# First-layer cross attention: where the exponentials and their sums are made

## The chip, the cores and the metric

The kernel runs on one core of a Trainium2 chip. A core has a matrix engine (PE, with PEld for its weight loads), VectorE (DVE), ScalarE (ACT), GpSimd (POOL) and SyncE (SP), which issues most transfers. Each engine works through its own instructions in order; semaphores hold an instruction back until its operands are there. The metric is the device time of one execution in microseconds.

## The reference

The model is a decoder of two layers over 32 sequences of 128 tokens, 128 features wide, with a context of 77 keys for each sequence. Layer 0 is retention, cross attention and a mixture of 8 experts; layer 1 is a memory, a differential cross attention and a second mixture. The change is in the cross attention of layer 0 alone. The reference cut to it:

```python
q = decoder_output @ wq_w + wq_b          # 16 heads of 8 features
k = encoder_output @ wk_w + wk_b
v = encoder_output @ wv_w + wv_b
score = jnp.einsum('bhqd,bhkd->bhqk', q, k) / jnp.sqrt(8.0)
score = score * mask
score = jnp.where(score == 0, NEG_INF, score)
alignment = jax.nn.softmax(score, axis=-1)
context = jnp.einsum('bhqk,bhkd->bhqd', alignment, v)
heads = context.reshape(b, -1, 128) @ wo_w + wo_b
```

## The kernel before, in words

All arithmetic is fp32. The 32 sequences are taken in eight groups of four (G = 4). The 77 keys are padded to S2 = 78 by repeating the last key, so that four heads of 78 keys make 312 columns, which fall into three strided parts of 104.

For one sequence the attention has two steps. `weigh(n)` (L528) works with the 128 queries on the partitions. GpSimd spreads the keys by head into `km` (L531). PE makes the scores `csc` of 16 heads in four products (L541). VectorE multiplies them by the mask into `ph` (named `prob` in the profile, 128 x 16 x 78, L543), makes the penalty `z` (L549), adds it (L550), takes the maximum over the keys for each query and head (`mx`, L552), and subtracts it (L553).

`read(n, ph)` (L556) turns that to keys on the partitions. PE makes 12 transposes of 104 x 128 into `ptp` (L564), and ScalarE takes the exponential on the way from PSUM to `pT`, two instructions of 104 x 768. `attend` (L488) then makes two sets of 12 products with `pT` (L494, each 32 rows of output): one with the values `vb` for the numerator, and one with the constant `vmask`, zeros and ones, for the sum of the exponentials. The sums are inverted by `power` (L155), a logarithm and an exponential on ScalarE, and VectorE multiplies (L574) into `oT`. The values and the mask both have a zero in the row of the repeated key.

`expln` (L149) is a helper through which the activations are issued, so all exponentials and logarithms have line L139 in the profile.

`cross0` (L576) runs these steps one sequence ahead: `weigh(n + 1)` is issued before `read(n)`. The stage is woven by `beside` (L1414) with other work: the retention (`retention`, L370) and query, key and value products (`prepare0`, L506) of groups ahead, and the output product, layer norms and routing (`joined0`, `route`) of the group behind, then the scatter of its tokens to the experts (`dispatch`, L646). The order on each engine is not the source's: a scheduler of the framework places the instructions by its own estimate of when each can run, so an edit to one step can move others.

Names in the trace that the steps below use: `yn` (L462) is the normed retention output; `po_ro` its product with the output weights; `ry` (L465) the sum with the input; `x` from `ry` (L317) the layer norm after it; `cqT` and `ckT` the queries and keys; `rqT` and `rkT` those of retention, `qm` (L391) GpSimd's spread of `rqT`, `rsc` the retention scores, `rt` (L411) the scores times the decay, `py` (L425) their product with the values and `yr` (L433) its copy; `xT_ln` a transposed layer norm; `place` (L664) the rows to which tokens are scattered; `pvc` (L475) the value products.

Tiles come from pools with few buffers. `prob` has three, which `ph` and `z` share; `pair` has two, and the scores, the transposes and the retention scores take turns in it. A step that holds one of these long keeps others from starting.

Of the kernel before, what the change touches and what calls it, by code (L numbers as in the profile page):

```python
# [10 lines left out]
F32 = mybir.dt.float32  # L11
I32 = mybir.dt.int32
U32 = mybir.dt.uint32
AF = mybir.ActivationFunctionType
ALU = mybir.AluOpType
AX = mybir.AxisListType

P = 128
B, S, D = 32, 128, 128
S2 = 78  # L20
# [7 lines left out]
KT = 26  # L28
# [81 lines left out]
def kernel(ctx: ExitStack, tc: tile.TileContext, a: dict, at: dict):  # L110
    nc = tc.nc
    cp = ctx.enter_context(tc.tile_pool(name="const", bufs=1))
    st = ctx.enter_context(tc.tile_pool(name="stream", bufs=2))
    wk = ctx.enter_context(tc.tile_pool(name="work", bufs=2))
    sm = ctx.enter_context(tc.tile_pool(name="small", bufs=4))
# [4 lines left out]
    def bank(name):  # L120
        return ps.tile([P, 512], F32, tag="bank", name=name)

    def pair(name):
        return pp2.tile([P, 2, 512], F32, tag="pair", name=name)

    def bank3(name):
        return bank(name).rearrange("p (b f) -> p b f", b=G)
# [4 lines left out]
    def by_table(table, out, x, func, **kw):  # L132
        if stretch["table"] != table:
            load = nc.scalar.add_instruction(
                mybir.InstLoadActFuncSet(name=nc.get_next_instruction_name(), act_func_set_id=table, ins=[], outs=[])
            )
            in_order(load, stretch["used"])
            stretch.update(table=table, load=load, used=[])
        act = nc.scalar.activation(out, x, func, **kw)  # L139
        in_order(act, [stretch["load"]])  # L140
        stretch["used"].append(act)
# [7 lines left out]
    def expln(out, x, func, **kw):  # L149
        by_table(EXP_LN, out, x, func, **kw)  # L150
# [4 lines left out]
    def power(out, x, p, bias=0.0):  # L155

        expln(out, x, AF.Ln, bias=bias)
        expln(out, out, AF.Exp, scale=p)
# [9 lines left out]
    def c_(name):  # L168
        return cst[:, at[name][0] : at[name][1]]
# [24 lines left out]
    def load_context(g):  # L194

        c4 = st.tile([P, G, 4, S2], F32, tag="c4", bufs=1, name=f"c4{g}")
        nc.sync.dma_start(c4, a["ctx4"][g])
        return c4
# [286 lines left out]

    vmask = c_("vmask").rearrange("p (t d) -> p t d", t=3)

    def attend(chunk, vb, num, den):  # L488

        for out, lhs in ((num, vb), (den, vmask)):  # L490
            for t in range(3):
                for j in range(4):
                    js = slice(32 * j, 32 * j + 32)
                    nc.tensor.matmul(  # L494
                        out[js, :],
                        lhsT=lhs[: 4 * KT, t, js],
                        rhs=chunk(j, t),
                        start=(t == 0),
                        stop=(t == 2),
                        skip_group_check=True,  # L500
                    )


    served = {}
# [23 lines left out]
    def weigh(n):  # L528
        qT, kT, _, mk, _ = served[n]
        km = wk.tile([P, 4, S2], F32, tag="km", name="km0")  # L530
        nc.gpsimd.tensor_tensor(  # L531
            km,
            kT.unsqueeze(1).broadcast_to([P, 4, S2]),
            c_("kmask0").unsqueeze(2).broadcast_to([P, 4, S2]),
            ALU.mult,
        )
        ph = wk.tile([P, 16, S2], F32, tag="prob", bufs=3, name="prob0")
        pscs = [pair("csc") for _ in range(2)]
        for r in range(4):
            rr = slice(32 * r, 32 * r + 32)  # L540
            nc.tensor.matmul(pscs[r // 2][:, r % 2, : 4 * S2], lhsT=qT[rr, :], rhs=km[rr, :, :], start=True, stop=True)  # L541
        for k in range(2):
            nc.vector.tensor_mul(  # L543
                ph[:, 8 * k : 8 * k + 8, :].rearrange("p (r h) k -> p r h k", r=2),
                pscs[k][:, :, : 4 * S2].rearrange("p r (h k) -> p r h k", h=4),
                mk.unsqueeze(1).unsqueeze(1).broadcast_to([P, 2, 4, S2]),
            )
        z = wk.tile([P, 16, S2], F32, tag="prob", bufs=3, name="z")
        nc.vector.tensor_scalar(z, ph, 0.0, NEG_INF, ALU.is_equal, ALU.mult)  # L549
        nc.vector.tensor_add(ph, ph, z)  # L550
        mx = sm.tile([P, 16], F32, tag="mx", name="mx0")
        begun.append(nc.vector.tensor_reduce(mx, ph, AX.X, ALU.max))  # L552
        nc.vector.tensor_tensor(ph, ph, mx.unsqueeze(2).broadcast_to([P, 16, S2]), ALU.subtract)  # L553
        return ph

    def read(n, ph):  # L556
        _, _, vb, _, oT = served.pop(n)
        pT = wk.tile([P, 2, 2, 3, S], F32, tag="pT", bufs=4, name="pT0")
        for k in range(2):
            pt = pair("ptp")  # L560
            for i in range(2):
                for t in range(3):
                    h0 = 8 * k + 4 * i
                    nc.tensor.transpose(  # L564
                        pt[: 4 * KT, i, t * S : (t + 1) * S],
                        ph[:, h0 : h0 + 4, :].rearrange("p h k -> p (h k)")[:, t::3],
                        ident,
                    )
            expln(pT[: 4 * KT, k].rearrange("p i t s -> p i (t s)"), pt[: 4 * KT, :, : 3 * S], AF.Exp)
        acc = bank3("pav0")  # L570
        attend(lambda j, t: pT[: 4 * KT, j // 2, j % 2, t, :], vb, acc[:, 0, :], acc[:, 1, :])
        rd = wk.tile([P, S], F32, tag="rd", name="rd0")
        power(rd, acc[:, 1, :], -1.0)
        nc.vector.tensor_mul(oT, acc[:, 0, :], rd)  # L574

    def cross0():  # L576

        ph = weigh(0)
        yield
        for n in range(B):  # L580
            ahead = weigh(n + 1) if n + 1 < B else None
            yield
            read(n, ph)
            yield
            ph = ahead
# [349 lines left out]
    def keys1(g, c4):  # L935
        pk = bank("dpk")[:, : G * S2]
        nc.tensor.matmul(pk, lhsT=w_("L1_xattn_Wk"), rhs=c4[:, :, 0, :], start=True, stop=True)
        kT = wk.tile([P, G, S2], F32, tag="ckT", name="dkT")
        nc.scalar.copy(kT, pk.rearrange("p (b k) -> p b k", b=G))
        yield  # L940
        km, vbs = [], []
        for b0 in range(0, G, 2):
            pair_km = wk.tile([P, 2, 8, S2], F32, tag="prob", bufs=3, name="km1")
            for i in range(2):
                nc.gpsimd.tensor_tensor(
                    pair_km[:, i],
                    kT[:, b0 + i, :].unsqueeze(1).broadcast_to([P, 8, S2]),
                    c_("kmask1").unsqueeze(2).broadcast_to([P, 8, S2]),
                    ALU.mult,
                )  # L950
                km.append(pair_km[:, i])
            for i in range(2):
                vbs.append(values(c4, b0 + i, 1))
            yield
        keyed[g] = km, vbs
# [420 lines left out]
    def after0(g, fine=False):  # L1376
        x2 = yield from joined0(g, held.pop(("x1", g)), held.pop(("oT", g)), fine)
        yield
        yield from route(g, x2, fine)
# [74 lines left out]
    last = [after0(NG - 1, True), dispatch(NG - 1, 1, other_tiles), keys1(0, load_context(0))]  # L1454
# [62 lines left out]
```

## Time and profile before

| | us |
|---|---|
| Median of 3 runs | 1583.14 |
| Lowest and highest | 1569.38 and 1587.96 |
| Profiled execution | 1564.15 |
| Its span, first to last instruction | 1562.3 |
| First exponential of the attention by key, start | 71.8 |
| Last product of `pav` in this attention, start | 544.2 |
| PE busy | 1221.8 |
| VectorE busy | 784.1 |
| ScalarE busy | 490.6 |
| GpSimd busy | 466.5 |

The profiled execution is some 19 us below the median. Each profile row names a line, an engine, an operation, the tile written and read, its shapes and a count, then busy microseconds and mean nanoseconds of one, then the idle time of the engine before it and what ended that. A matrix product in fp32 appears as two records. Times in the time line count from the start of the span.

### The profile page before, as it was taken

Reading aid. Unit: us, or ns where it says so; the run is one execution under the profiler, and the core shown is the slowest. Engines: PE = TensorE matmul, PEld = TensorE weight load, DVE = VectorE, ACT = ScalarE, POOL = GpSimd, SP = SyncE. Lnnn points to the kernel's source line nnn. Section 1 sums busy time; section 2 is a strip of 40 time slices with the busy share of each in tenths; the row PEclk is TensorE's granted clock in tenths of the full one; section 3 lists DMA queues with packets and bytes.
Section 4 is the critical chain, followed back from the end, with each engine's and each line's share of the span. In section 5 each row is a group of like instructions: output and inputs, shape, how many; then the busy total and the mean of one; then the engine's idle time right before and its main releaser. Section 6 shows DMA issues by size and latency. Waiting matters only on the chain.

```text
span 1562.3 us, 27821 instructions
## 1 busy us (share of the span) xinstructions
PE 1221.8 (78%) x11445; PEld 910.3 (58%) x11445; DVE 784.1 (50%) x2174; ACT 490.6 (31%) x1036; POOL 466.5 (30%) x451
## 2 busy tenths in 40 slices
PE   4788777778777789899796998888989999527840
PEld 3556555555555578788674665656666666316430
DVE  2678767676576734222333435535445354376212
ACT  3235243332334424233231232432424334200113
POOL 0110131321214465554635303123011010004762
PEclk8798788776788689899895788988989999656975
DMA  3322221120211235455521101011011000001335
GB/s 113 105 75 76 75 76 53 64 89 21 75 48 65 91 125 174 148 181 186 155 87 46 38 2 51 22 42 44 30 48 30 23 15 16 14 0 25 68 31 121
DMA packets 75599, 107.21 MB, mean 69 GB/s; under 512 B 13840, under 2 KB 60944, under 8 KB 75472
## 3 DMA queue, kind: packets, MB, share of 16 engines
q0 software_dynamic: 19088, 53.63, 12.1%
q1 hardware_dynamic: 56384, 51.80, 10.7%
q8 instruction: 90, 1.47, 0.4%
q14 instruction: 37, 0.30, 0.1%
HBM read 65.80 MB, written 39.60 MB: 67 GB/s over the span
## 4 chain that ended last, share of the span: by engine, by line
PE 52%; DVE 19%; issue 9%; POOL 8%; ACT 5%; DMA 4%; another core or an unknown queue 3%; POOLq 0%; SPq 0%; ACTq 0%; DVEq 0%
PE pgu L810 6%; PE pav L1015 5%; PE dsc L963 5%; PE dst L987 4%; PE dst L998 3%; PE pav L494 3%; PE pd L825 3%; PE pvc L475 3%; PE ptp L564 2%; POOL total L1331 2%; PE csc L541 2%; DVE top L965 2%; DVE x L320 2%; PE py L425 2%
## 5 line engine op out<-in xcount | busy, mean ns | idle before, releaser
L965 DVE TENSOR_REDUCE top<-dsc 128x4 f32<-128x312 f32 x256 | 111.5, 476 | 139.8 <-PE dsc L963 128.3
L139 ACT ACTIVATE pT<-dst 104x768 f32<-104x768 f32 x128 | 96.5, 806 | 237.9 <-PE dst L998 224.1
L810 PE MATMUL pgu<-tT,wt 128*128 128x256 f32 x624 | 152.6, 391 | 7.0 <-ACT tT L792 6.3
L963 PE MATMUL dsc<-km,dqT 32*128 32x312 f32 x512 | 121.4, 520 | 31.7 <-DVE top L965 22.5
L810 PEld LDWEIGHTS pgu<-tT,wt 128*128 128x128 f32 x624 | 116.3, 195 | 25.5 <-ACT tT L792 11.7
L816 DVE TENSOR_TENSOR sg<-sg,pgu 128x512 f32<-128x512 f32 x78 | 53.5, 686 | 151.6 <-ACT sg L139 142.3
L987 PE MATMUL dst<-dqT,km 32*104 32x128 f32 x1536 | 119.2, 337 | 7.1 <-ACT pT L139 6.3
L671 POOL DMA_INDIRECT xslot<-z,place x64 | 70.2, 1097 | 146.2 <-DVE place L664 107.0
L987 PEld LDWEIGHTS dst<-dqT,km 32*104 32x104 f32 x1536 | 98.6, 228 | 20.5 <-ACT pT L139 11.1
L825 PE MATMUL pd<-wt,sg 128*128 128x128 f32 x624 | 88.7, 288 | 16.6 <-DVE sg L816 12.0
L963 PEld LDWEIGHTS dsc<-km,dqT 32*128 32x128 f32 x512 | 50.3, 200 | 85.7 <-DVE top L965 49.2
L564 PE MATMUL ptp<-cst,prob 128*104 128x128 f32 x384 | 74.2, 342 | 32.5 <-DVE gbi L457 23.8
L825 PEld LDWEIGHTS pd<-wt,sg 128*128 128x128 f32 x624 | 81.7, 200 | 22.3 <-DVE sg L816 15.4
L998 PE MATMUL dst<-mT,cst 32*104 32x128 f32 x1536 | 87.6, 299 | 2.9 <-issue 2.9
L531 POOL TENSOR_TENSOR km<-ckT,cst 128x312 f32<-128x312 f32 x32 | 22.7, 720 | 216.4 <-PE csc L541 151.0
L564 PEld LDWEIGHTS ptp<-cst,prob 128*104 128x104 f32 x384 | 60.3, 189 | 41.5 <-issue 34.6
L998 PEld LDWEIGHTS dst<-mT,cst 32*104 32x104 f32 x1536 | 78.3, 185 | 4.5 <-issue 4.4
L139 ACT ACTIVATE sg<-pgu 128x512 f32<-128x512 f32 x78 | 46.6, 597 | 97.7 <-PE pgu L810 80.1
L541 PE MATMUL csc<-km,cqT 32*128 32x312 f32 x256 | 61.1, 560 | 18.8 <-POOL km L531 13.0
L475 PE MATMUL pvc<-wv,c 128*104 128x128 f32 x384 | 69.0, 336 | 5.3 <-DVE top L965 3.9
L475 PEld LDWEIGHTS pvc<-wv,c 128*104 128x104 f32 x384 | 63.7, 242 | 14.2 <-DVE top L965 8.5
L857 POOL DMA_INDIRECT two<-xslot,place x64 | 61.9, 968 | 32.0 <-issue 16.3
(351 smaller groups left out, 2450.3 us busy)
## 6 DMA issues: line engine op xcount, KB each, us to landing
xslot<-zero SPq DMA_DIRECT2D x75, 256.0 KB
c<-in_ctx SPq DMA_DIRECT2D x16, 624.0 KB
wt<-in_experts SPq DMA_DIRECT2D x16, 192.0 KB
xg<-in_x SPq DMA_DIRECT2D x8, 256.0 KB
accrow<-fh SPq DMA_DIRECT2D x8, 256.0 KB
facc<-accrow SPq DMA_DIRECT2D x8, 256.0 KB
xrow<-x SPq DMA_DIRECT2D x8, 256.0 KB
total<-x SPq DMA_DIRECT2D x8, 256.0 KB
```

The costliest lines, as they stand in the source:

```text
L139: act = nc.scalar.activation(out, x, func, **kw)
L475: nc.tensor.matmul(pv[: 4 * KT, t, :], lhsT=c4[:, b].rearrange("p h k -> p (h k)")[:, t::3], rhs=wv[:, layer, :], start=True, stop=True,)
L541: nc.tensor.matmul(pscs[r // 2][:, r % 2, : 4 * S2], lhsT=qT[rr, :], rhs=km[rr, :, :], start=True, stop=True)
L564: nc.tensor.transpose(pt[: 4 * KT, i, t * S : (t + 1) * S], ph[:, h0 : h0 + 4, :].rearrange("p h k -> p (h k)")[:, t::3], ident,)
L671: put = nc.gpsimd.indirect_dma_start(out=xslot, out_offset=bass.IndirectOffsetOnAxis(ap=place[:, k, g * G + b : g * G + b + 1].bitcast(U32 ...
L810: nc.tensor.matmul(pgu[:, i, c * TB * P : (c + 1) * TB * P], lhsT=w[:, at_w : at_w + P], rhs=x, start=True, stop=True)
L825: nc.tensor.matmul(pd[:, b, :], lhsT=sgs[c0 // 2][:, c, b, :], rhs=w[:, at_w : at_w + D], start=(c0 + c == 0 and b == 0), stop=(c0 + c == ...
L963: nc.tensor.matmul(banks[w][:, : 4 * S2], lhsT=qT[rr], rhs=km[rr, 4 * k : 4 * k + 4, :], start=True, stop=True)
L965: nc.vector.tensor_reduce(tops[n % 3][:, w, 4 * k : 4 * k + 4], banks[w][:, : 4 * S2].rearrange("p (h k) -> p h k", h=4), AX.X, ALU.max,)
L987: nc.tensor.matmul(pts[w // 2][: 4 * KT, w % 2, t * S : (t + 1) * S], lhsT=km[rr, 4 * k : 4 * k + 4, :].rearrange("p h k -> p (h k)")[:, t ...
L998: nc.tensor.matmul(pts[w // 2][: 4 * KT, w % 2, t * S : (t + 1) * S], lhsT=fold[rr], rhs=mT[rr, :], start=False, stop=(t == 2), skip_group ...
L1015: nc.tensor.matmul(out[js], lhsT=lhs[: 4 * KT, t, js], rhs=pTs[j % 2][: 4 * KT, :, j // 2, t, :], start=(t == 0), stop=(t == 2), skip_grou ...
```

## The change

The exponentials are taken before the transposes, with the queries still on the partitions. VectorE negates the maxima. ScalarE then makes one exponential for each head, 128 x 77, in place, with the negated maximum as the bias and the sum over the keys as a second output. VectorE inverts the 16 sums of each query and multiplies the weights by them. The transposed weights are then only copied from PSUM by ScalarE. `attend` makes one set of 12 products, with the values; the set with `vmask` is gone here, though the second layer still has one. ScalarE copies the result to `oT`. The 78th column, the repeated key, is not exponentiated and stays a scaled score; it meets a zero row in the values.

```diff
-    def attend(chunk, vb, num, den):
-        for out, lhs in ((num, vb), (den, vmask)):
-            for t in range(3):
-                for j in range(4):
...
+    def attend(chunk, vb, out):
+        for t in range(3):
+            for j in range(4):
...
-        nc.vector.tensor_tensor(ph, ph, mx.unsqueeze(2).broadcast_to([P, 16, S2]), ALU.subtract)
+        nc.vector.tensor_scalar(mx, mx, -1.0, None, ALU.mult)
+        last = S2 - 1
+
+        sums = sm.tile([P, 16], F32, tag="sums0", name="sums0")
+        for h in range(16):
+            expln(ph[:, h, :last], ph[:, h, :last], AF.Exp, bias=mx[:, h : h + 1], accum_out=sums[:, h : h + 1])
+        nc.vector.reciprocal(sums, sums)
+        nc.vector.tensor_mul(ph, ph, sums.unsqueeze(2).broadcast_to([P, 16, S2]))
         return ph
...
-            expln(pT[: 4 * KT, k].rearrange("p i t s -> p i (t s)"), pt[: 4 * KT, :, : 3 * S], AF.Exp)
-        acc = bank3("pav0")
-        attend(lambda j, t: pT[: 4 * KT, j // 2, j % 2, t, :], vb, acc[:, 0, :], acc[:, 1, :])
-        rd = wk.tile([P, S], F32, tag="rd", name="rd0")
-        power(rd, acc[:, 1, :], -1.0)
-        nc.vector.tensor_mul(oT, acc[:, 0, :], rd)
+            nc.scalar.copy(pT[: 4 * KT, k].rearrange("p i t s -> p i (t s)"), pt[: 4 * KT, :, : 3 * S])
+        acc = bank("pav0")[:, :S]
+        attend(lambda j, t: pT[: 4 * KT, j // 2, j % 2, t, :], vb, acc)
+        nc.scalar.copy(oT, acc)
```

More of the change, by code (lines that the diff above doesn't have):

```diff
@@ L486 @@
     vmask = c_("vmask").rearrange("p (t d) -> p t d", t=3)
-    def attend(chunk, vb, num, den):
-        for out, lhs in ((num, vb), (den, vmask)):
-            for t in range(3):
-                for j in range(4):
[L493 to L501, printed above, removed]
+    def attend(chunk, vb, out):
+        for t in range(3):
+            for j in range(4):
+                js = slice(32 * j, 32 * j + 32)
+                nc.tensor.matmul(
+                    out[js, :],
+                    lhsT=vb[: 4 * KT, t, js],
+                    rhs=chunk(j, t),
+                    start=(t == 0),
+                    stop=(t == 2),
+                    skip_group_check=True,
+                )
     served = {}
```

## The prediction

> **What bounds the kernel now.** I read first where first-layer attention lies (the windows by stage), then the chain that ended last inside it, then the groups of instructions that the edit touches, and last one group of four sequences in order of time, because only that shows what a longer step on ScalarE would push.
>
> The windows cut the stage at the row maxima of successive groups; columns are length, then busy time of PE, PEld, DVE, ACT and POOL, granted clock, DMA share, GB/s.
>
> ```profile
> 183.80:248.00 64.20, 48.60 (x474) 35.75 (x474) 47.14 (x126) 25.03 (x59) 17.26 (x16) 0.85 0.22 71
> 248.00:317.00 69.00, 53.28 (x472) 38.85 (x472) 47.48 (x122) 24.79 (x59) 17.82 (x16) 0.77 0.20 66
> ...
> sum 488.00, PE 378.32 PEld 276.12 DVE 353.10 ACT 181.55 POOL 122.02; mean PE 54.05 PEld 39.45 DVE 50.44 ACT 25.94 POOL 17.43
> ```
>
> The stage runs from 58 to 546 us: 488 us for 32 sequences. PE is busy 78% of it, VectorE 72%, ScalarE 37%. No engine is full; the stage is a chain that hops between PE, VectorE and ScalarE. The groups that the edit touches or that price it:
>
> ```profile
> L139 ACT ACTIVATE pT<-ptp 104x768 f32<-104x768 f32 x64 | 50.4, 804 | 59.7 <-PE ptp L564 59.2 <-PE pt_ln L346 0.5
> L553 DVE TENSOR_TENSOR prob<-prob,mx 128x1248 f32<-128x1248 f32 x32 | 46.9, 1466 | 0.4
> L494 PE MATMUL pav<-pT,vb 104*32 104x128 f32 x768 | 39.8, 327 | 0.8 <-ACT pT L139 0.7
> L494 PE MATMUL pav<-pT,cst 104*32 104x128 f32 x768 | 34.7, 306 | 0.0
> L317 ACT ACTIVATE x<-ry,nb_l0a,r_l0a 128x128 f32<-128x128 f32 x32 | 13.2, 482 | 2.2 <-DVE mv_l0x L308 1.7 <-DVE nb_l0a L312 0.5
> L139 ACT ACTIVATE rd<-rd 128x128 f32<-128x128 f32 x32 | 9.8, 307 | 0.8
> L350 ACT COPY xT_c<-pt_c 128x512 f32<-128x512 f32 x16 | 9.3, 584 | 24.9 <-PE pt_c L346 24.6
> L139 ACT ACTIVATE rd<-pav 128x128 f32<-128x128 f32 x32 | 8.9, 277 | 121.9 <-PE pav L494 95.4 <-PE pvc L475 14.2 <-remote 12.3
> L976 ACT COPY mT<-pt_mx 128x128 f32<-128x128 f32 x32 | 8.4, 263 | 8.3 <-PE pt_mx L974 8.3
> ```
>
> Here ScalarE waits for PE (121.9 us before rd alone), not the reverse. In the chain inside 58 to 546 us, L494 is the largest line, 10.2% (50 us). Half of its products are the mask products (pav<-pT,cst). One group, in order of time:
>
> ```profile
> 246.46 1.45 DVE L552 TENSOR_REDUCE mx<-prob 128x16 f32<-128x1248 f32 x1
> 251.79 1.64 ACT L462 ACTIVATE yn<-yr,gbi,gsc 128x128 f32<-128x128 f32 x4
> 260.57 1.65 ACT L317 ACTIVATE x<-ry,nb_l0a,r_l0a 128x128 f32<-128x128 f32 x4 [0.29 <-DVE mv_l0x L308]
> 266.05 0.99 POOL L671 DMA_INDIRECT xslot<-z,place  x1 [22.53 <-DVE place L664]
> 285.73 0.57 ACT L379 COPY rqT<-pq 128x512 f32<-128x512 f32 x1
> 288.52 1.45 DVE L552 TENSOR_REDUCE mx<-prob 128x16 f32<-128x1248 f32 x1
> ```
>
> Call its sequences A to D. ScalarE carries the layers woven in beside them: yn and x (the next groups), rqT and the key and value copies (retention two groups on). All are on the way to PE's next work.
>
> **The change, part by part.** *Removed:* 768 mask matmul records, 34.7 us of PE busy, 1.1 per sequence; they stand on the chain, so at most 25 us (half of 50). The subtraction, 1.466, is replaced by a multiplication of one shape, also taken as 1.466. rd's two activations (0.277 + 0.307) and the 0.28 product give way to one 128x128 copy from PSUM, 0.263 by L976. The wide Exp becomes a copy of one shape: 0.80 before; the copy rows L976 and L350 rise 0.836 ns per element, so 0.80 after.
>
> *Added, small:* a negation and a reciprocal of 128x16 on VectorE; the nearest rows are its 128x4 and 128x8 ones, 0.15 to 0.2 each. Less the product gone, VectorE's sum hardly moves.
>
> *Added, large:* 16 Exp of 128x77 per sequence with a pointer for the bias and an accumulator. L317 gives the form nearest: four in a row take 1.65, one 0.482, so the pitch is (1.65-0.482)/3 = 0.389. Take off 51 elements (0.043) and the second pointer (0.08, from 128x4 rows with and without one, 0.287 and 0.201): 0.267. No row has an accumulator. The lower bound is 0.267, a free one. Upper: no overlap (0.287 + 73 x 0.836 ns = 0.348) plus a small instruction to fetch the sum (0.2): 0.55. I take 0.42, between them, since the sum exists only after the last element: 0.348, no overlap, and 0.07 for handing it over. That is 6.7 us per sequence, 215 in all, and brings ScalarE to about 390 of 488 us.
>
> The Trainium skill, "ScalarE: Activation LUTs", section "What ACT_TABLE_LOAD costs", states 280 ns plus 0.833 per element with a pointer, and 93 ns overlap: 0.251 here. It speaks against sixteen narrow instructions, most of each being fixed cost, but names no price for the accumulator. By its 0.251 the sum below ends at -19 us (a gain); by my 0.42 at +35. Rows here agree with the formula at 0.267; the difference is the accumulator.
>
> **What lies beside and what on the path.** In the changed order VectorE runs A's maximum, B's mask, z and maximum, and only then A's reciprocal and multiplication, so most of A's exponentials are covered there. But ScalarE is in order, and what stands behind each block waits. I walk the group with 0.42, in the changed order of each engine:
> - A's block runs 248.3 to 255.0. yn is behind it: 256.7 instead of 253.4 at its end. po_ro, then ry, 258 instead of 256.6.
> - B's first ten stand before r_l0a: x starts 262.6 instead of 260.6; six more lie among the two layer norms, so the context keys end 268.6 instead of 265.7. VectorE's place is +3.3, hence POOL's eight scatters and the key products queued behind them (276.9 before) begin 3 us later. SP's zero fills are released by the maxima and its order hardly moves.
> - A's copies of the transposes come only after B's block: products for A end 273, C's scores follow, C's maximum ends 281.2 instead of 274.6. This lateness is partly absorbed, for D's scores stood behind POOL in the kernel before.
> - C's block runs 283.6 to 290.3. Behind it is rqT, 290.9 instead of 286.3, then POOL's qm and PE's rsc. D's maximum ends 295.5 instead of 290.0, the rt pair 298 instead of 293.7.
> - D's block runs 297.1 to 303.8; behind it yr, xT_ln and C's copies, to 306.6. The mask products that filled 303.3 to 305.2 here are gone. The second rt pair ends 313 instead of 308.6.
>
> So a group is 4.4 us longer, with the removed products already out. Eight groups: +35 us. About 2.5 of the four blocks lie on the path, so 0.01 us on each Exp is 0.4 us per group, 3.2 us in all. At 0.267 the sum is 35 - 0.153 x 320 = -14; at 0.55 it is 35 + 0.13 x 320 = +77. The later stages (experts, second attention) keep their instructions; the start of the stage and its end, where experts join, are counted as groups like the others.
>
> The profiled execution took 1564.15 us (span 1562.3); with the sum, about 1599. The median shown is 1583.14, 19 above it, so the forecast for the median is 1583 + 35 = 1618. 1% is 16 us, about what a measurement of this kernel can tell from no change.
>
> **The rivals.**
> 1. *ScalarE becomes the bound* (0.2). The accumulator costs an instruction of its own, 0.55 each: 282 us more, 453 busy of 488, and all four waits bite. For: yn, rqT, yr and the copies stand behind blocks. Against: 306 us of idle time now. +77: 1660.
> 2. *Faster* (0.18). The accumulator is nearly free and the exponentials fit in ScalarE's idle time; then only the 25 us of mask products and the rd chain leave the path. For: ScalarE idles 63% here and PE's L494 leads the chain. It decides from a pitch of 0.31 downward (35/3.2 = 11 hundredths below 0.42). At 0.267: 1583 - 14 = 1569; with more slack at POOL's waits, down to -25: 1558.
> 3. *Nothing measurable* (0.22). The blocks cost what the products gave, at a pitch of 0.31 to 0.36: 1583 to 1599.
> 4. *The forecast* (0.4): 1618, itself within about 1600 to 1640.
>
> The range must reach into 1 and 2: 1567 to 1670. Faster 0.18, same 0.22, slower 0.6.
>
> **What would show it.** Right: the stage at about 523 us; ScalarE busy near 390 in it; a spacing of about 0.42 between exponentials; yn, rqT and yr waiting on nothing but their own engine; PE's wait for ScalarE (yn, xT_ln, rqT through qm) grown, the mask products' 34.7 us gone. Wrong: a spacing under 0.31, or VectorE's reciprocal held long by ScalarE in every sequence (then more than 2.5 blocks are on the path), or a longer time in the second attention.

## The result, and the profile after

The changed kernel takes 1665.49 us (median of four executions, 1662.38 to 1674.73), against 1578.59 for the kernel before on the same chip: a ratio of 1.0626 [1.0579, 1.0672], some 87 us more. The forecast of +35 us (1618) had the sign, and the time lies inside the range of 1567 to 1670, but the size is far out. On three other chips the same kernel came out 1.0424, 1.0433 and 1.0461 of the kernel before, which itself takes about 1537 us there: 63 to 70 us more. So the experiments below are each compared with what ran on the same chip. On the chip of x1, x3 and x5 two executions of the kernel before were slow ones and are left out of every comparison.

The first row of the page after, and the stage that was 58 to 546 us before (length, then busy time of PE, PEld, DVE, ACT and POOL, granted clock, DMA share, GB/s). It now ends at 643, where the first expert products start:

```profile
span 1673.0 us, 27258 instructions
PE 1247.6 (75%) x10677; PEld 912.1 (55%) x10677; DVE 808.4 (48%) x2206; ACT 653.3 (39%) x2028; POOL 460.8 (28%) x451
```

```profile
58.00:643.00 585.00, 392.99 (x2736) 270.57 (x2731) 379.12 (x921) 344.62 (x1417) 116.66 (x113) 0.68 0.17 55
```

The first expert product (`pgu`) started at 545.9 us before and starts at 642.3 now, 96 us later. The two executions differ by 110.7 us of span, more than the medians do, for the one before lies below all its timed runs and the one after is the slowest of its four. So most of the loss is in this stage. What lies behind it is 14 us longer (1016.4 and 1030.7 us), 13 of them in the second attention (518 and 531 us), with the same instructions. This part is not the edit's: in three traces from one other chip, everything behind the stage takes 982 and 988 us in two variants of the kernel before (x4, x6) and 979 in the changed kernel (after_again).

PE has 757 records fewer in the stage (2736 for 3493) and yet 15 us more of busy time, at a granted clock of 0.68 for 0.79. ScalarE is busy 345 us; the prediction said about 390.

The exponentials in the groups of ScalarE for this stage (busy, mean ns of one, then the idle time before them):

```profile
L139 ACT ACTIVATE prob<-prob,mx 128x77 f32<-128x77 f32 x512 | 176.5, 354 | 20.8 <-DVE mx L552 20.8
L139 ACT ACTIVATION_READ_ACCUMULATOR prob<-prob,mx 128x1 f32 x512 | 100.2, 196 | 0.0
L575 ACT COPY pT<-ptp 104x768 f32<-104x768 f32 x64 | 50.2, 799 | 48.1 <-PE ptp L570 46.0 <-remote 2.0
```

The sum over the keys is an instruction of its own in the records, 196 ns. The time line of the profiled execution (start, duration) shows how it costs less than that:

```profile
257.01 1.44 DVE L551 TENSOR_REDUCE mx<-prob 128x16 f32<-128x1248 f32 x1
262.09 0.36 ACT L139 ACTIVATE prob<-prob,mx 128x77 f32<-128x77 f32 x1
262.35 0.19 ACT L139 ACTIVATION_READ_ACCUMULATOR prob<-prob,mx 128x1 f32 x1
262.44 0.35 ACT L139 ACTIVATE prob<-prob,mx 128x77 f32<-128x77 f32 x1
...
267.25 0.36 ACT L139 ACTIVATE prob<-prob,mx 128x77 f32<-128x77 f32 x1
267.78 0.58 ACT L379 COPY rqT<-pq 128x512 f32<-128x512 f32 x1
268.44 1.04 POOL L391 TENSOR_TENSOR qm<-rqT,cst 128x512 f32<-128x512 f32 x1 [0.28 <-ACT rqT L379]
...
273.84 1.44 DVE L551 TENSOR_REDUCE mx<-prob 128x16 f32<-128x1248 f32 x1
275.21 1.21 DVE L411 TENSOR_TENSOR rt<-rsc,dmat 128x1024 f32<-128x1024 f32 x1
276.34 0.64 DVE L552 TENSOR_SCALAR mx<-mx 128x16 f32<-128x16 f32 x1
277.01 0.36 ACT L139 ACTIVATE prob<-prob,mx 128x77 f32<-128x77 f32 x1 [1.41 <-DVE mx L552]
...
282.17 0.36 ACT L139 ACTIVATE prob<-prob,mx 128x77 f32<-128x77 f32 x1
282.65 0.25 DVE L558 RECIPROCAL sums<-sums 128x16 f32<-128x16 f32 x1 [4.54 <-ACT prob L139]
```

From one exponential to the next it is 0.344 us (262.09 to 267.25 is fifteen of them): the next one starts before the accumulator is read out. A block of 16 takes 5.5 us, not 6.7. The rest of the fence is what the walk of the prediction looked for: rqT stands behind a block and GpSimd's qm behind rqT; at the end VectorE's reciprocal has waited for the block. And something the walk did not have: the fourth sequence's maxima end at 275.28, but the negation stands behind a retention product (`rt`, 1.21 us) on VectorE, so its block starts only at 277.01.

The chain of this stage by line, and four of its waits (total us, times, longest), both of the kernel after:

```profile
by line: ACT prob L139 18.9%; PE csc L540 9.7%; PE pav L493 7.9%; PE ptp L570 6.6%; ACT x L317 3.6%; DVE mx L551 3.5%; DVE prob L542 3.4%; PE rsc L401 3.3%; PE py L425 3.2%; PE pvc L475 2.8%; DVE rt L411 2.6%; DVE prob L549 2.6%; PE po_ro L
```

```profile
DVE sums L558 <- ACT prob L139: 51.2, 17, 5.8
PE po_ro L360 <- ACT yn L462: 48.3, 7, 7.8
POOL qm L391 <- ACT rqT L379: 24.1, 6, 19.7
PE py L425 <- DVE rt L411: 35.6, 12, 5.9
```

Before, the leading line of this chain was PE's L494 with 10.2%; now ScalarE's exponentials lead it with 18.9%. VectorE waits for whole blocks (17 times, up to 5.8 us), and PE's output product of the retention waits for yn, which stands behind a block, 7 us in each of seven groups. In the kernel before, only its weight load is listed as waiting for yn, and shortly:

```profile
PEld po_ro L360 <- ACT yn L462: 5.1, 7, 0.8
```

### The profile page after: what moved, and what is told of

Its sections match the earlier page's. It is cut to its first block, busy times and chain, and to the rows that moved or that the text cites. A ratio compares the mean times of both kernels' runs of the same rounds, so it can differ in the third digit from the quotient of the medians.

```text
span 1673.0 us, 27258 instructions
## 1 busy us (share of the span) xinstructions
PE 1247.6 (75%) x10677; PEld 912.1 (55%) x10677; DVE 808.4 (48%) x2206; ACT 653.3 (39%) x2028; POOL 460.8 (28%) x451
## 4 chain that ended last, share of the span: by engine, by line
PE 54%; DVE 16%; ACT 13%; issue 7%; POOL 5%; DMA 3%; another core or an unknown queue 2%; POOLq 0%; SPq 0%; ACTq 0%; DVEq 0%
ACT prob L139 7%; PE pav L1019 5%; PE pgu L814 5%; PE dsc L967 5%; PE dst L991 4%; PE dst L1002 4%; PE csc L540 3%; PE pav L493 3%; PE pd L829 3%; PE pvc L475 3%; PE ptp L570 2%; POOL total L1335 2%; DVE x L320 2%; DVE top L969 2%
## 5 line engine op out<-in xcount | busy, mean ns | idle before, releaser
L139 ACT ACTIVATE prob<-prob,mx 128x77 f32<-128x77 f32 x512 | 176.5, 354 | 20.8 <-DVE mx L552 20.8
L570 PE MATMUL ptp<-cst,prob 128*104 128x128 f32 x384 | 80.9, 367 | 44.9 <-DVE prob L559 22.4
L829 PE MATMUL pd<-wt,sg 128*128 128x128 f32 x624 | 88.7, 288 | 17.6 <-DVE sg L820 14.7
L139 ACT ACTIVATION_READ_ACCUMULATOR prob<-prob,mx 128x1 f32 x512 | 100.2, 196 | 0.0
L570 PEld LDWEIGHTS ptp<-cst,prob 128*104 128x104 f32 x384 | 64.1, 195 | 59.4 <-issue 29.2
L542 DVE TENSOR_TENSOR prob<-csc,mk 128x624 f32<-128x624 f32 x64 | 50.6, 804 | 60.0 <-PE csc L540 55.7
L475 PE MATMUL pvc<-wv,c 128*104 128x128 f32 x384 | 70.2, 338 | 3.9 <-DVE top L969 3.9
```

Of the source, the lines that this page charges most:

```text
L475: nc.tensor.matmul(pv[: 4 * KT, t, :], lhsT=c4[:, b].rearrange("p h k -> p (h k)")[:, t::3], rhs=wv[:, layer, :], start=True, stop=True,)
L570: nc.tensor.transpose(pt[: 4 * KT, i, t * S : (t + 1) * S], ph[:, h0 : h0 + 4, :].rearrange("p h k -> p (h k)")[:, t::3], ident,)
L829: nc.tensor.matmul(pd[:, b, :], lhsT=sgs[c0 // 2][:, c, b, :], rhs=w[:, at_w : at_w + D], start=(c0 + c == 0 and b == 0), stop=(c0 + c == ...
```

## The experiments

**The parts by themselves.** x4 takes the removal alone: the kernel before without mask products, logarithm, exponential and multiplication of the sums.

```diff
-        for out, lhs in ((num, vb), (den, vmask)):
+        for out, lhs in ((num, vb),):
...
-        power(rd, acc[:, 1, :], -1.0)
-        nc.vector.tensor_mul(oT, acc[:, 0, :], rd)
+        nc.scalar.copy(oT, acc[:, 0, :])
```

> The kernel before with the mask products, the reciprocal and its multiplication left out (the numerator is only copied). It measures what the removed part is worth by itself. By the prediction's step (half of what the chain shows for these products): 20 to 30 us faster, 1550 to 1560. If, as putting them back into the changed kernel suggests, they lie in PE's slack: within 10 us of before.

1509.39 us against 1537.74 on the same chip: 0.9828 [0.9766, 0.989], 28 us less, as expected. The first step of the sum (at most 25 for the products, and what the chain of the sums gives) stands. So the added part costs more than the whole loss shows: if the two parts simply add, 63 + 28 = 91 us on this chip.

x6 does the opposite: it leaves the kernel before as it is and puts ScalarE's new work beside it, on constants that nobody reads.

```diff
+        for h in range(16):
+            expln(junk, zero[:, :77], AF.Exp, bias=mx[:, h : h + 1], accum_out=jsum[:, h : h + 1])
```

> The kernel before with sixteen more exponentials with sums per sequence, of constants, with the maximum as bias, into tiles that nothing reads: ScalarE does the added work, but no transposes wait for it. If ScalarE's in-order queue (what stands behind the blocks) is what costs, most of the 85 us: 1630 to 1660. If it is the weights' longer way (maximum, exponentials, multiplication, transposes), 1585 to 1610.

1569.4 us, 1.0193 [1.0137, 1.0248]: 32 us, at the upper end of the second theory. A full extra load of ScalarE, which the weights themselves do not pass through, costs about a third of 91. The load is even larger than in the changed kernel: where these exponentials follow each other directly, it is 0.48 us from one to the next here, for 0.344 there. They all write one tile, and whether that is the reason was not tried. The framework also spreads these instructions between others, so this is not the price of the load in the places it has in the changed kernel. By subtraction, then, most of the loss is the weights' own longer way; the next two runs test that directly.

x3 keeps that way but takes the block down to one instruction of 128x1248; x2 keeps sixteen instructions and takes only the sums from them. The first part of the diff is x3's, the second x2's.

```diff
-        for h in range(16):
-            expln(ph[:, h, :last], ph[:, h, :last], AF.Exp, bias=mx[:, h : h + 1], accum_out=sums[:, h : h + 1])
-        nc.vector.reciprocal(sums, sums)
+        expln(ph, ph, AF.Exp, bias=mx[:, 0:1])
+        nc.vector.reciprocal(sums, mx)
...
-            expln(ph[:, h, :last], ph[:, h, :last], AF.Exp, bias=mx[:, h : h + 1], accum_out=sums[:, h : h + 1])
-        nc.vector.reciprocal(sums, sums)
+            expln(ph[:, h, :last], ph[:, h, :last], AF.Exp, bias=mx[:, h : h + 1])
+        nc.vector.reciprocal(sums, mx)
```

> The changed kernel with one exponential of 128x1248 per sequence instead of sixteen, with the negated maximum of the first head as bias for all; the sums are left out (the reciprocal is taken of the maxima instead). The hand-overs from VectorE to ScalarE and back stay, the block falls from 5.5 to about 1.3 us. Theory 1 and 2 (the block's length): the stage loses more than it gained, 1545 to 1575, with a clock near 0.79. Theory 3 (the hand-overs themselves and the weights' longer way, not the block): 1600 or more.

> The changed kernel with the sixteen exponentials without their sums (left out; the reciprocal is taken of the maxima). A block should fall from 5.5 us (0.343 each) to about 4.0 (0.25 each). If the length of the blocks sets the time (one exponential of about 1.3 us gave 1550, sixteen with sums 1665, so 27 us per us of block), 1620 to 1635. If the number of the hand-overs or the number of instructions counts and not their length, 1650 or more.

x3 takes 1549.92 us, 0.9854 [0.9778, 0.9931] of the kernel before on its chip: level, within the intervals, with the products simply removed (x4, 0.9828). Its one instruction, in the groups of its ScalarE:

```profile
L139 ACT ACTIVATE prob<-prob,mx 128x1248 f32<-128x1248 f32 x32 | 42.6, 1333 | 10.7 <-DVE mx L552 8.6 <-issue 2.1
```

So an exponential in this place costs nothing beyond the interval, some 12 us, if it is 1.3 us long. (In x3 the negation of the fourth sequence of a group no longer stands behind `rt`, except in the earliest, so its fall from the changed kernel is not the block's alone.)

x2 takes 1557.5 us, 1.0135 [1.0068, 1.0202], and the changed kernel on the same chip (after_again) 1600.91. The sums alone are worth 43 us, within the fall of 30 to 45 (from 1665) that the theory of the block's length gave. The order is no rival here, for the negation of the fourth sequence of a group stands behind `rt` in x2 as well. A block of x2 in its time line:

```profile
251.52 4.10 ACT L139 ACTIVATE prob<-prob,mx 128x77 f32<-128x77 f32 x16
```

(4.10 - 0.35)/15 = 0.25 us from one to the next. So the sum costs 0.094 us on each exponential, 1.5 us on a block and 48 us on 32 of them, of which 43 are seen at the end.

> The changed kernel again, beside the others on one chip: 1655 to 1675.

It came out at 1600.91 us, 1.0424 [1.0359, 1.0488], below what the first chip gave; the excess of about 20 us there came with that chip, and what causes it was not found.

**Is it PE's clock?** With the products gone PE has more idle time in the stage and its records are slower (a score product 628 ns for 560). x5 puts work into that idle time: a bank of PSUM set apart, and 24 unread products ahead of `po_ro` in every fourth sequence. x5_filled_0 sets the bank apart and fills nothing. x1 puts the mask products back, unread. The first part of the diff is x5_filled_24's, the second x1's.

```diff
+        for _ in range(24 if n % 4 == 1 else 0):
+            fill = nc.tensor.matmul(warm[:, :P], lhsT=ident, rhs=dmat[:, 0, :], start=True, stop=True)
+            in_order(fill, [neg])
...
-        attend(lambda j, t: pT[: 4 * KT, j // 2, j % 2, t, :], vb, acc)
-        nc.scalar.copy(oT, acc)
+        attend(lambda j, t: pT[: 4 * KT, j // 2, j % 2, t, :], vb, acc[:, 0, :])
+        attend(lambda j, t: pT[: 4 * KT, j // 2, j % 2, t, :], vmask, acc[:, 1, :])
+        nc.scalar.copy(oT, acc[:, 0, :])
```

> The changed kernel with one PSUM bank set apart (three in turn instead of four) and no filling: the comparison for the filled one. Both theories: 0 to 20 us above the changed kernel, 1665 to 1685, for the lost bank.

> The changed kernel with one PSUM bank set apart and 24 products of 128x128 in it that nothing reads, in every fourth sequence, on PE just ahead of the retention output product, where PE waits some 7 us for the normed retention output behind a block of exponentials. Theory 1 (clock): the filled wait keeps the clock up for the products behind it; useful PE work gets faster and the time is 8 to 25 us below the same kernel without filling, although PE has about 40 us more to do. Theory 2 (waits alone): equal to that kernel within 5 us, or longer.

> The changed kernel with the 12 products with the mask put back for each sequence, into columns of the accumulator that nothing reads. Theory 1 (clock): the changed kernel is slower than forecast because PE, waiting for ScalarE's blocks, is granted a lower clock (0.68 in the stage against 0.79); more products fill PE, the clock rises to 0.71 or more, and the time stays within 10 us of the changed kernel: 1655 to 1675. Theory 2 (the waits behind the blocks alone, the clock plays no part): the products cost what they were taken to give, some 25 us: about 1690.

x5_filled_0 takes 1658.06, x5_filled_24 1685.42. The filling did go where it was meant: the products are there, and `po_ro` waits less for yn.

```profile
L556 PE MATMUL warm<-dmat,cst 128*128 128x128 f32 x384 | 51.3, 300 | 0.0
L362 PE MATMUL po_ro<-wm,yn 128*128 128x128 f32 x56 | 14.3, 345 | 16.8 <-ACT yn L464 16.8
```

In x5_filled_0 the same row reads:

```profile
L362 PE MATMUL po_ro<-wm,yn 128*128 128x128 f32 x56 | 14.1, 425 | 48.3 <-ACT yn L464 48.3
```

The wait fell by 31.5 us (48.3 to 16.8) for 51.3 us of filling, and the mean clock of the stage rose from 0.72 to 0.76; yet the time went up by 27, as the theory of the waits has it. The filling overshot its hole by 20 us, which is most of that; but it gave little back. PE's other work up to the first expert product is 374 us busy for 377. So filling the idle time ahead of `po_ro` does not make PE's other products faster here. (The profiled execution of x5_filled_24 was its fastest, 1670.02 us, so the trace holds only some 10 of the 27 us.)

x1 takes 1647.43 us, 1.0486 [1.0407, 1.0564] on its chip: less than the changed kernel's 1.0626 on the first, with more to do, and less than either theory gave. Side by side on one chip:

> The changed kernel once more, so that the three others of this call can be set against it on one chip: 60 to 90 us above before.

> The changed kernel with the mask products put back unread, now on the same chip as the changed kernel. If PE's clock or its idle time is what the products decide, 0 to 20 us below the changed kernel; if the products are plain cost, as leaving them out of the kernel before gave 28 us, 15 to 30 us above it.

1604.76 and 1575.36 us: 29 us less with the products put back, more than expected. They also change the order in which the framework places other instructions. In x1 the fourth sequence's negation comes right after its maxima, in all groups but the earliest; in the changed kernel it stands behind `rt`. Clock and order are thus two possible causes of one number, and the series with y3 and y5 takes them apart.

**Ends or middle?** In the trace of the result the opening (to the sixth sequence's maxima) is 29 us longer, the five groups after it 49 together, the closing 18. The prediction counted all groups alike. y1 makes the change for sequences 5 to 25 only (shown), y2 for the eleven others, each with the kernel before's form for the rest.

```diff
+    def changed(n):
+        return 5 <= n <= 25
...
+        if not changed(n):
+            nc.vector.tensor_tensor(ph, ph, mx.unsqueeze(2).broadcast_to([P, 16, S2]), ALU.subtract)
+            return ph
```

> The change for the 21 sequences between, the ends as before. If the ends hold half of the loss: 30 to 48 us above before. If every sequence costs alike: 40 to 60 us, two thirds of the changed kernel's loss.

> The change for eleven sequences alone (the first five and the last six); the other 21 as before. The traces lay half of the stage's growth (48 of 97 us) on these ends, where little is woven in beside a block. If so, this kernel is half of the changed kernel's loss above before: 30 to 48 us. If every sequence costs alike, as the prediction counted, 11 of 32, a third: 20 to 30 us.

y1: 1571.29 us, +33.8, or 1.61 for each changed sequence. y2: 1557.01, +19.5, or 1.77 for each. Neither total lies in the range of equal cost (40 to 60, 20 to 30); both are below it. But for each changed sequence the two agree within their intervals (some 0.4 us each way), so the ends are no worse than the middle. What is missing to the whole change's 67 on this chip (14 us) comes only when both are changed, and why was not found. The half of the loss that the trace shows at the ends is thus not made by the sequences there.

**The order.** y3 lets ScalarE make the negation, right ahead of its exponentials. y5 does that with the mask products put back too.

```diff
-        nc.vector.tensor_scalar(mx, mx, -1.0, None, ALU.mult)
+        nc.scalar.mul(mx, mx, -1.0)
```

> The changed kernel once more, as the base of the three others on the same chip: 1.042 to 1.063 of the kernel before.

> The changed kernel with the negation of the maxima made by ScalarE, right ahead of its exponentials, so that the fourth sequence's block no longer stands behind a retention product on VectorE; nearly all else keeps its order. Theory of the order: the waiting negation is the bulk of what the put-back mask products gained, so 18 to 29 us below the changed kernel. Theory of the clock: the negation is only worth its own delay, 1.3 us in each of eight groups less 0.3 us of ScalarE's in each of 32 sequences, so 0 to 10 us below.

> The negation by ScalarE and the mask products put back (computed, not read). Theory of the order: with the negation out of the way already the products gain nothing more, so as y3_negation_by_scalar or up to 15 us above it, by their 35 us of matrix engine. Theory of the clock: they gain again, 15 to 30 us below y3_negation_by_scalar.

After_fourth 1607.68, y3 1586.77, y5 1581.16 us; ratios to the kernel before 1.0461 [1.0422, 1.0499], 1.032 [1.028, 1.036], 1.0291 [1.0258, 1.0324]. The negation, which takes 0.16 us in 27 of its 32 records (0.65 in the other five, one of them shown below), is worth 21 us when it moves to another engine. The fourth sequence of one group in the time line, first of the changed kernel (after_fourth), then of y3:

```profile
268.48 1.44 DVE L551 TENSOR_REDUCE mx<-prob 128x16 f32<-128x1248 f32 x1
269.84 1.21 DVE L411 TENSOR_TENSOR rt<-rsc,dmat 128x1024 f32<-128x1024 f32 x1
270.97 0.65 DVE L552 TENSOR_SCALAR mx<-mx 128x16 f32<-128x16 f32 x1
271.54 1.21 DVE L411 TENSOR_TENSOR rt<-rsc,dmat 128x1024 f32<-128x1024 f32 x1
271.66 0.36 ACT L139 ACTIVATE prob<-prob,mx 128x77 f32<-128x77 f32 x1 [1.41 <-DVE mx L552]
```

```profile
264.00 1.44 DVE L551 TENSOR_REDUCE mx<-prob 128x16 f32<-128x1248 f32 x1
265.36 2.34 DVE L411 TENSOR_TENSOR rt<-rsc,dmat 128x1024 f32<-128x1024 f32 x2
265.67 0.20 ACT L552 ACTIVATE mx<-mx 128x16 f32<-128x16 f32 x1
265.91 0.36 ACT L139 ACTIVATE prob<-prob,mx 128x77 f32<-128x77 f32 x1
```

From the maxima's end to the first exponential it is 1.74 us in the one and 0.47 in the other. But the group is shorter by more than that difference of 1.3: from these maxima to the next sequence's it is 28.2 us against 25.0. The windows show where the rest is: first the stretch with the block, then the one with the products behind it, again after_fourth first, y3 second.

```profile
271.20:278.00 6.80, 5.67 (x48) 4.22 (x48) 2.21 (x4) 6.34 (x34) 0.39 (x1) 0.64 0.44 151
278.00:284.30 6.30, 6.00 (x48) 3.78 (x48) 4.23 (x32) 2.06 (x5) 0.00 (x0) 0.62 0.01 3
```

```profile
266.50:272.40 5.90, 5.69 (x48) 4.33 (x48) 2.01 (x4) 5.90 (x33) 0.61 (x1) 0.55 0.51 178
272.40:276.50 4.10, 3.94 (x49) 2.69 (x48) 3.69 (x29) 1.90 (x5) 0.00 (x0) 1.00 0.02 4
```

The second stretch holds the same 48 product records in both (a 49th at the edge of y3's), 6.0 us of PE at a granted clock of 0.62 against 3.9 at 1.00. In the same place of the next three groups the clock reads 0.67, 0.55 and 0.60 against 0.99, 1.00 and 1.00. The 0.62 is a mean: cut finer, the clock is 0.50 or 1.00. In after_fourth it is full for 3.4 us and half again behind that; in y3 it is full for 6.8 us.

```profile
276.10:279.50 3.40, 2.01 (x19) 1.67 (x17) 1.86 (x4) 3.40 (x12) 0.00 (x0) 1.00 0.00 0
279.50:284.30 4.80, 4.76 (x40) 2.67 (x36) 3.04 (x31) 0.56 (x3) 0.00 (x0) 0.50 0.01 3
```

```profile
271.80:278.60 6.80, 5.01 (x60) 3.42 (x60) 6.29 (x34) 2.50 (x5) 0.00 (x0) 1.00 0.01 2
```

In the full 3.4 us of after_fourth lies a wait of PE of 1.4 us (up to 278.26) for the transposed layer norm, which y3's earlier block takes away. So order and clock are one story here: the late block costs 1.3 us in a group, and about 2 us more because the products behind it run slowly. What switches the clock was not tried; that the wait does it is only argued. The Trainium skill, "TensorE: Matmul & The Clock Gate", section "Why this matters for your kernels", asks for no idle gap of PE over about 3 us. The gap here is 1.4 us, but in seven groups PE waits for yn as well, 48.4 us in all and up to 7.9 at once. Filling most of such waits, as the rule would have it, left PE's other products about as slow as they were (374 us for 377, x5). No run here tests the figure of 3 us itself.

With the negation out of the way, the put-back products still gain 5.6 us rather than cost their own time. This was between the two theories and is little more than the spread of four executions (y3's lie between 1581.76 and 1591.18); its cause stays open.

**Sums by query in another form.** What loses could be the sums by query as such, or only sixteen narrow instructions. y4 takes one exponential with the maximum over all heads of the query as its bias, sums it by head on VectorE, and applies the inverted sums at the end: they are transposed once by PE.

```diff
+        begun.append(nc.vector.tensor_reduce(mx[:, 0:1], ph.rearrange("p h k -> p (h k)"), AX.X, ALU.max))
...
+        expln(ph, ph, AF.Exp, bias=mx[:, 0:1])
+        nc.vector.tensor_reduce(sums, ph[:, :, :last], AX.X, ALU.add)
+        nc.vector.reciprocal(rs, sums.unsqueeze(2).broadcast_to([P, 16, 8]))
...
+        nc.tensor.transpose(acc[:, 1, :], rs.rearrange("p h d -> p (h d)"), ident)
...
+        nc.scalar.copy(rd, acc[:, 1, :])
+        nc.vector.tensor_mul(oT, acc[:, 0, :], rd)
```

> Sums by query as in the changed kernel, but one exponential of 128x1248 for each sequence, with the maximum over all heads of a query as its bias; VectorE sums it by head, inverts the sums into 128x128, PE transposes these once, and they multiply the product with the values at the end instead of the weights ahead of the transposes. If the loss is the sixteen instructions of 5.5 us on the path, this lies below the kernel before: its block is 1.25 us, the subtraction is gone, the sum (1.45 us of VectorE) takes the place of the multiplication but nobody on the path waits for it: 0.965 to 0.99 of the kernel before. If sums by query lose as such (VectorE's work between the scores and the transposes), 1.01 to 1.04.

1539.87 us, 1.0019 [0.9993, 1.0044]: level with the kernel before, and 68 us below the changed one. It lies between the two theories: the sums by query as such do not lose, but the gain did not come. That VectorE's added work eats it is argued from its groups (here those of y4_again), and y6 tests it; an inversion takes 0.946 us and waits 13 us in all for PE to read its single buffer:

```profile
L557 DVE TENSOR_REDUCE sums<-prob 128x16 f32<-128x1232 f32 x32 | 45.7, 1427 | 3.8 <-ACT prob L139 3.8
L559 DVE RECIPROCAL rs<-sums 128x128 f32<-128x128 f32 x31 | 29.3, 946 | 13.4 <-PE pav L578 13.3
```

y6 changes three things at once: it inverts 128x16, lets ScalarE spread the result into two buffers, and lets ScalarE make the negation.

```diff
-        nc.vector.tensor_scalar(mx[:, 0:1], mx[:, 0:1], -1.0, None, ALU.mult)
+        nc.scalar.mul(mx, mx, -1.0)
...
-        nc.vector.reciprocal(rs, sums.unsqueeze(2).broadcast_to([P, 16, 8]))
+        nc.vector.reciprocal(sums, sums)
+        nc.scalar.copy(rs, sums.unsqueeze(2).broadcast_to([P, 16, 8]))
```

> The base of y6_sums_by_transpose_narrow on the same chip: 0.999 to 1.005 of the kernel before.

> As y4_sums_by_transpose, but VectorE inverts only 128x16 (0.2 us for 0.95), ScalarE spreads that to 128x128 into two buffers instead of one, and ScalarE makes the negation. If VectorE's 24 us and the wait for the buffer lie on the path: 0.98 to 0.99 of the kernel before, and 15 to 24 us below y4_sums_by_transpose. If y4 is held by the products and scatters as the kernel before is: 0.995 to 1.005.

y4_again 1540.07; y6 1517.1 us, 0.9885 [0.9843, 0.9928]: 23 us below y4, and 18 us below the kernel before, a small gain (1.2%), but one whose interval does not reach 1. The changed kernel was not run on this chip; from its 1601 to 1608 us on the three others like it, y6 is an estimated 85 us faster. Which of the three changes gave how much was not separated. Its rows on VectorE, on ScalarE, and its stage up to the first expert product:

```profile
L557 DVE TENSOR_REDUCE sums<-prob 128x16 f32<-128x1232 f32 x32 | 45.8, 1431 | 11.1 <-ACT prob L139 11.0
L558 DVE RECIPROCAL sums<-sums 128x16 f32<-128x16 f32 x32 | 7.7, 241 | 0.0
```

```profile
L139 ACT ACTIVATE prob<-prob,mx 128x1248 f32<-128x1248 f32 x32 | 42.7, 1334 | 0.6
L560 ACT COPY rs<-sums 128x128 f32<-128x128 f32 x32 | 9.5, 298 | 16.3 <-DVE sums L558 8.3 <-DVE lg L631 5.1 <-DVE place L673 2.9
```

```profile
58.00:533.00 475.00, 364.34 (x2757) 249.45 (x2758) 349.20 (x914) 227.84 (x489) 110.69 (x112) 0.79 0.21 68
```

The exponentials' idle time ahead of them fell from 17.6 us in y4_again to 0.6, VectorE's busy time in the stage from 371 us to 349, and the stage is 475 us long, for 497. One caution belongs to y4 and y6: with one maximum for all heads, a head whose scores lie far enough below the others' would lose its sum to underflow. The weights of this model are 0.02 wide, so that its scores lie close together; a kernel for arbitrary weights would have to keep a maximum for each head.

## Why the prediction was right or wrong

*The mask products and their chain: right.* Up to 25 us was said for the products; with their chain 28 are measured (x4, interval 17 to 36).

*The cost of one exponential: too high.* 0.42 was taken between 0.267 and 0.55; it is 0.344. Without the sum it is 0.25 (x2), and here the Trainium skill's formula ("ScalarE: Activation LUTs", "What ACT_TABLE_LOAD costs", 0.251) was closer than the 0.267 that I made of the rows. The 0.55 of the first rival was built on an instruction that fetches the sum; that instruction exists and lasts 0.196, but all except 0.094 of it is hidden. ScalarE did not become the bound: 345 busy of 585 us.

*The cover of the blocks: wrong, and this is the step that failed.* With a pitch of 0.344 the prediction's own sum would have been 35 - 0.076 x 320 = +11 us, in the case "nothing measurable", against +63 to +87. "Most of A's exponentials are covered" and "about 2.5 of the four blocks lie on the path", 3.2 us for each hundredth on every exponential, are what the walk said. x2 against after_again gives 43 us for 9.4 hundredths: 4.6 us each, so about 3.6 of four blocks: these last hundredths had almost no cover. And as a mean over the whole block: the walk had 4.4 us for a group with the products' 25/8 = 3.1 already taken out, so 7.5 of its 26.8 us of blocks, 1.9 for each sequence; 4.8 of each block's 6.7 us had cover. Measured is 91/32 = 2.9 on the path of a block of 5.5 (0.7 of it for the late negation, 21/32): the cover is 2.6 us, about half.

Three things in the walk made the sum come out at +35. First, its result was compared with the one group it had walked, 69.0 us from maxima to maxima, where the mean of five groups of the kernel before is 66.7: 2.3 us a group, 18 in all. The walked group was to be 69.0 + 4.4 = 73.4 us; the mean of the same five groups is 73.5 in after_fourth and 76.6 in the first trace. So the length of the group was met on one chip, and it was the base that was off. That it was met was luck, for two errors cancelled in it. The walk did not have the negation behind `rt`: 21 us in all (y3). And it took the block 1.2 us too long: with 5.5 it gives 73.4 - 2.5 x 1.2 = 70.4, and y3, in which the negation no longer stands on VectorE, has 70.2. (The kernel before was not traced on these faster chips. x4's stage ends at 520.6 us on one of them; if its 28 us all lie in the stage, that of the kernel before would end near 549 there, an estimate, much as the 545.9 of its trace.) Put right in these three, the sum is 35 + 18 + 21 - 8 x 3 = 50 us, against 63 to 70 on three chips; the rest, 13 to 20 us there and 37 on the first, stays open.

*PE's durations taken from before: wrong.* The products behind a late block ran at a granted clock of about 0.6 (after_fourth) where they run at 1.00 in y3, and in the first trace the stage's mean fell from 0.79 to 0.68. The 2 us a group that y3 gets back this way are within its 21 us. How much more the lower clock costs in other places, and whether it makes the 20 us by which the loss is larger on the first chip, is not settled.

*Start and end counted like other groups: right*, by y1 and y2 (1.61 and 1.77 us for each sequence).

*What would show it.* The wait of PE for yn grew as said. VectorE's reciprocal was held by ScalarE in 17 of 32 sequences; the prediction had named "in every sequence" as the sign that more than 2.5 blocks are on the path, so that sign came by half. A longer second attention, also named, is in the trace but not the edit's. Of the rivals, "faster" did not miss by 0.034 of pitch (0.344 for 0.31), because the slope was wrong as well: x2, with no sums and 0.25, where the prediction's sum gives a gain of 19 us, is still at 1.0135.

## What to carry to other kernels

Count the work put between two engines by how it lengthens the chain, and give it cover only where another instruction can be named for the whole time: here half of each block was covered, not seven tenths. Compare a walk with the mean period, not with the period that was walked. A small instruction that starts a long block (here a negation of 0.16 us) belongs on the engine of the block, and sums by row were cheaper here from one wide instruction and one reduction (y4, y6) than from sixteen narrow ones with an accumulator, where one maximum for all heads will do.

## What the runs showed of the hardware

- An exponential with an accumulator leaves a second record, 196 ns, which overlaps the next exponential: 0.344 us from one to the next with it, 0.25 without (128x77, bias by pointer).
- The same stretch of 48 product records took 6.0 us at a granted clock of 0.62 and 3.9 at 1.00, in two kernels that differ in one small instruction on another engine (y3). Cut finer, the clock in these stretches is 0.50 or 1.00. More work on PE came out faster than less in one pair (1575.36 for 1604.76) and slower in another (1685.42 for 1658.06).
- Chips differ: the kernel before took 1579 and 1571 us on two of them and 1535 to 1538 on four others. The changed kernel lost 87 us on the first of these, and 63 to 70 on three of the latter. That difference of the kernel before lies behind the stage: the traces before and after and those of x1, x3 and x5, whatever the variant, have 1016 to 1045 us there, all others 972 to 993.
